# Opening of a two-layer graph attention kernel: four score row buffers, conversions placed behind the ids, first adjacency loads of the second phase in row buffers, and later loads in the first phase's loop

## The chip, the cores and the metric

The kernel runs on one core of a Trainium2 chip. The metric is the device time of one execution in microseconds, as the median of several runs. The engines are TensorE (PE in the profile, its weight loads PEld), VectorE (DVE), ScalarE (ACT), GpSimd (POOL) and SyncE (SP, which here only issues DMAs).

## The reference

Two graph attention layers over 4096 nodes share one adjacency matrix. Its entries are drawn with probability 1/256, made symmetric, and every node is its own neighbour. Cut to what matters:

```python
def reference(x, adj, W_heads, a1, a2, W_out, b_out, W, a):
    # layer 0: 8 heads of 128
    Wh = einsum('nf,hfd->hnd', x, W_heads)
    e = leaky_relu(s1[:, :, None] + s2[:, None, :], 0.2)   # s1 = Wh.a1, s2 = Wh.a2
    att = softmax(where(adj > 0, e, NEG))
    feat = elu(einsum('hnm,hmd->hnd', att, Wh))            # heads side by side
    x = layernorm(x + feat @ W_out + b_out)
    # layer 1: 4 heads of 64, the same form, no output matrix
    ...
    return layernorm(x + h_prime)
```

x is 4096 x 256 in float32, adj is 4096 x 4096 in int32 (64 MB).

## The kernel before, in words

Layer 0 uses that the adjacency is sparse. The 256 groups of 16 target nodes are taken in 8 phases of 32 groups (GP); a phase is 512 rows of adj. For each phase the kernel finds which nodes are neighbours of any target of a group, as lists of ids, and then gathers only those nodes' rows from a table in memory.

The table has one row per node: the 256 numbers of x, a one, two factors per head that come from the node's score (16 numbers), and 32 words. A word says, as a bit mask, which of the 16 targets of one group have this node as a neighbour. There are two tables, and phase s uses table s % 2. The numbers of x are copied into a table by `inputs` (L546, four DMAs of 1 MB, L549). The other 49 words of each row are written by `publish` (L701, DMA L703) from the tile `tail`.

Making a phase's ids has two parts:

- `words_of(s)` (L554) loads the phase's 512 rows of adj in 16 pieces of 512 KB (`load`, DMA L572), converts each to signs in bf16 (`convert`; on DVE for phase 0, L582, on ACT for the others, L584), and sums them with bit weights on PE (`count`, L596), which gives the words. Two buffers hold converted pieces. Phase 0's pieces are loaded into the gather's row buffers (tag "G", 6 buffers), later phases' into three buffers of their own (`aq`). `words_of` returns a list of 19 steps for the later phases; a step loads piece m, converts piece m - 2 and counts piece m - 3.
- `lists_of(s)` (L626) turns the words and picks out the largest candidate numbers, eight at a time (`take`, L673 and L674), merges the four quarters (`merge`, `more`), fills the lists (`fill`, whose copy on ACT is L733), transposes them (`turn`, L738) and writes the tile `ids` (`number`, L751). It returns a list of pieces with a cost each.

The score factors come from class `Scores`. `chunk(k)` makes six steps for each quarter of the nodes: scores on PE (L378), `factors` on DVE and ACT into the tile `row` (L418, L422, L425), transposes of it (`turn`, L433), and `store`. `store` (L439) writes two halves of `row` to the tensor r_d with DMAs issued on ACT (L443), copies the transposed scores (L448, L453), and makes the table's factors on ACT (L454, L457). The publication (L703, on ACT for phase 0) follows. There is one `row` buffer.

Everything up to the end of layer 0 is issued in the order in which the code is written, engine by engine (`manual_schedule`). `opening` (L791) builds phase 0's words and runs phase 0's pieces of `lists_of`; from piece 16 on it takes one score step behind each piece, and behind pieces 24, 26, 31, 33, 35 and 37 one step of the second phase's words (the queue `firsts`). So these loads and conversions stand between the pieces that lead to the ids. Then the first gathers are issued and the loop over groups starts at L1209.

In the loop, group n gathers the rows of group n + 5 (`gather`, L882 on POOL, four DMAs of 128 rows), weighs its own rows on DVE (`weigh`: L987 to L1002, into four buffers with tag "e"), and multiplies on PE (`gathered`, L1010). One more gather per four groups fetches rows shared by them (class `Shared`, L897), and every eight groups the tile of their own rows and score rows is loaded on SP (class `Near`, L940 and L944). Between these the loop takes

- two steps of `firsts` a group; when they are out, `turn_phase(1)` puts the second phase's pieces on the queue `picks`;
- from group 10 (FIRST_COUNT) of phase 0 one step a group of the third phase's words (the queue `counts`); from group 4 (COUNT) in later phases;
- pieces from `picks` as far as a budget per group allows (FIRST 3.0, later EXTRA 2.5, less what the group itself is reckoned at); what is left in group 24 of a phase is run at once;
- in group 27 of each phase `turn_phase` for the phase after next;
- in groups 5, 9, 13 and 17 the copies of x into the second table.

Layer 1 then runs densely over all pairs, bounded by PE. It is not touched by the change.

Of the kernel before, what the change touches and what calls it, by code (L numbers as in the profile page):

```python
# [9 lines left out]
F32 = mybir.dt.float32  # L10
# [8 lines left out]
P = 128  # L19
# [243 lines left out]
def fast_path(  # L263
# [34 lines left out]
    NB = NQ0  # L298
# [37 lines left out]
    class Scores:  # L336
# [29 lines left out]
        def chunk(self, k, src):  # L366
# [41 lines left out]
            def factors():  # L408
                if k == 0:
                    nc.vector.tensor_copy(self.mx[:, 0:1], held["pm"])  # L410
                    nc.vector.tensor_scalar(
                        self.mx[:, 1:2], self.mx[:, 0:1], -1.0, None, ALU.mult
                    )
                ps = held["ps"]
                row = held["row"] = small.tile(
                    [P, HC], F32, tag="row", name=f"row_{n}_{k}", bufs=1
                )
                nc.vector.tensor_scalar(  # L418
                    row[0 : 2 * DQ], ps[0 : 2 * DQ], self.mx[0 : 2 * DQ, 0:1], SPREAD,
                    ALU.add, ALU.min,  # L420
                )
                nc.scalar.activation(  # L422
                    row[2 * DQ :], ps[2 * DQ :], AF.Identity, bias=self.mx[2 * DQ :, 1:2]
                )
                nc.scalar.activation(  # L425
                    row[0 : 2 * DQ], row[0 : 2 * DQ], AF.Exp, scale=1.0 - SLOPE
                )
# [118 lines left out]
    def inputs(i, k):  # L546
        if k == 0:
            nc.sync.dma_start(table[i][N : N + 1, :], zero)
        nc.sync.dma_start(table[i][ts(k, CH), 0:F], x[ts(k, CH), :])  # L549

    lists = [None] * NPH
    words = {}

    def words_of(s):  # L554

        pw = []
        raw, bins = {}, {}
        HN = QN // 2
        NW = PT * NQ0
        PQ = NQ0 // 2  # L560

        def load(m):

            k, t, q = m // (PT * PQ), m // PQ % PT, m % PQ
            if s == 0:
                G = gpool.tile([P, NB, RW], F32, tag="G", name=f"Ga_{m}")
                v = G.rearrange("p b w -> p (b w)")[:, 0 : 2 * HN].bitcast(I32)
                raw[m] = v.rearrange("p (a n) -> p a n", a=2)
            else:
                raw[m] = apool.tile([P, 2, HN], I32, tag="aq", name=f"aq_{s}_{m}")  # L570
            queue = nc.scalar if s == 0 and m % 2 else nc.sync
            queue.dma_start(  # L572
                raw[m],
                adj[ts(s * PT + t, P), ts(k * PQ + q, 2 * HN)].rearrange(
                    "p (a n) -> p a n", a=2
                ),
            )

        def convert(m):
            mb = two.tile([P, 2, HN], BF16, tag="mb", name=f"mb_{s}_{m}", bufs=2)  # L580
            if s == 0:
                nc.vector.tensor_scalar(mb, raw.pop(m), 0.0, 0.5, ALU.is_gt, ALU.subtract)  # L582
            else:
                nc.scalar.activation(mb, raw.pop(m), AF.Sign, bias=half[:, 0:1])  # L584
            bins[m] = mb

        def count(m):


            k, t, q = m // (PT * PQ), m // PQ % PT, m % PQ  # L590
            if t + q == 0:
                pw.append(ps_0.tile([P, HN], F32, tag="o2", name=f"pw_{s}_{k}", bufs=1))
            mb = bins.pop(m)
            for a in range(2):
                r = ts(2 * q + a, GP)
                nc.tensor.matmul(  # L596
                    pw[k][r, :],
                    word[:, t, :],
                    mb[:, a],
                    start=(t == 0),  # L600
                    stop=(t == PT - 1),
                    tile_position=(0, (2 * q + a) * GP),
                    skip_group_check=True,
                )
            if t == PT - 1 and q == PQ - 1:
                if k == 0:
                    words[s] = two.tile([P, QN], F32, tag="ws", name=f"ws_{s}", bufs=2)

                nc.scalar.activation(
                    words[s][:, ts(k, HN)],  # L610
                    pw[k],
                    AF.Identity,
                    bias=half[:, 1:2],
                    scale=1.0 if s == 0 else 0.5,
                )

        lag = 5 if s == 0 else 2

        def piece(m):
            for f, mm in ((load, m), (convert, m - lag), (count, m - lag - 1)):  # L620
                if 0 <= mm < NW:
                    f(mm)

        return [lambda m=m: piece(m) for m in range(NW + lag + 1)]
# [166 lines left out]
    def opening():  # L791
# [19 lines left out]
        for k, (scores, pull, top, factors, turn, store) in enumerate(chunks):  # L811
# [3 lines left out]
            scored.add(turn, lambda k=k, store=store: (store(), publish(k, NCH)))  # L815
            if k == 0:
                scored.add(lambda: near.update({0: Near(0)}))
        firsts.add(*words_of(1))
        for m, (cost, piece) in enumerate(pieces[:-2]):
            piece()  # L820
            if m == 2:
                sc0.weights(a0_sb, w0T_sb)
                chunks[0][0]()
            elif m > 15:
                scored.some()

            if m in (24, 26, 31, 33, 35, 37):
                firsts.some()
        picks.add(*pieces[-2:])
        return firsts  # L830

# [337 lines left out]
    EXTRA = 2.5  # L1169
    FIRST = 3.0  # L1170
    COUNT = 4
    FIRST_COUNT = 10
    rows, shared, near, sums, means = ({} for _ in range(5))
    counts, picks = Late(), Late()

# [19 lines left out]
    with tc.manual_schedule():  # L1195
# [10 lines left out]
        shared[0].copy(near[0].rb)  # L1206
        shared[0].split()
        shared[0].weigh()
        for n in range(NG + SOON + 1):  # L1209
            i, o, s = n // GT, n % GP, n // GP  # L1210
            busy = 0.0
            if n < NG:
                if n == 2:
                    nc.sync.dma_start(w_sb, w0f.rearrange("(c p) d -> p c d", p=P))
                elif n == 4:
                    nc.sync.dma_start(wo_sb, w_out.rearrange("(h d) f -> d h f", d=D0))
                    nc.sync.dma_start(b_sb, b_out)
                if o == (COUNT if s else FIRST_COUNT) and s + 2 < NPH:
                    counts.add(*words_of(s + 2))
                if o == GP - AHEAD - 3:  # L1220
                    while picks.items:
                        picks.items.pop(0)[1]()
                if o == GP - AHEAD and s + 2 < NPH:
                    counts.all()
                    turn_phase(s + 2)
                if n % SL == 0 and n + 2 * SL < NG:
                    shared[n // SL + 2] = Shared(n // SL + 2)
                if n + AHEAD < NG:
                    rows[n + AHEAD] = gather(n + AHEAD)
                if n % GT == 0:  # L1230
                    if i + 1 < NT:
                        near[i + 1] = Near(i + 1)
                    aT = two.tile([P, KC, H0, P], F32, tag="aT", name=f"aT_{i}")
                if n % 4 == 1 and 0 < n // 4 <= NCH:
                    inputs(1, n // 4 - 1)
            if SOON <= n < NG + SOON:
                po, to = sums.pop(n - SOON)
                invert(n - SOON, po)
# [345 lines left out]
```

## Time and profile before

| | us |
|---|---|
| median of 3 runs | 2545.72 (2536.66 to 2552.91) |
| the profiled execution | 2237.41 |
| its span | 2235.6 |
| first gather (L897) starts | 85.67 |
| last gather (L882) starts | 1476.9 |

In the span PE is busy for 89%, DVE for 87%, ACT for 39% and POOL for 48%; the mean granted TensorE clock is 0.957. The profiled execution is shorter than the runs that are timed.

How to read the lines. In a timeline a line gives the start and the time in us, the engine, the source line, the operation, what it writes and reads with the shape, and how many were merged; in square brackets stands how long the engine had been idle before it and what ended that. A group line gives count, busy time, mean ns of one, and the idle time before. An engine's name with a q (ACTq, SPq) is its queue issuing a DMA. POOL's gathers are issued by the engine itself.

### The profile page before, as it was taken

What the parts mean: (1) busy time and instruction counts of PE and PEld (TensorE: products, weight loads), DVE (VectorE), ACT (ScalarE), POOL (GpSimd) and SP (SyncE); (2) the same over time, 40 slices, a digit from 0 to 9 for tenths busy, and PEclk for the clock granted to TensorE, in tenths of its full rate; (3) what the DMA queues carried; (4) which work ended last, traced back from release to release, by engine and by line L of the source; (5) the groups of instructions that cost most, each with busy time, mean ns of one, the idle gap of its engine ahead of it and who ended that gap; (6) DMA issues with size and microseconds to landing.
All of it is one profiled execution on the core that took longest, in us unless ns stands there. A gap on an engine that the chain in (4) does not pass through costs nothing.

```text
span 2235.6 us, 35623 instructions
## 1 busy us (share of the span) xinstructions
PE 1996.7 (89%) x12481; PEld 1142.5 (51%) x12481; DVE 1955.2 (87%) x4117; ACT 882.9 (39%) x1826; POOL 1077.9 (48%) x1154
## 2 busy tenths in 40 slices
PE   5487888989989999989888899888999999999996
PEld 2255566666666666666665667664424333333332
DVE  6579899999989999988999988747998899999996
ACT  1333424424334334334432233234445444465563
POOL 1377777777777777777777777730000000000000
PEclk9589999989999999999999999999999999999998
DMA  9799677578567677667665555538665566676762
GB/s 323 192 297 258 180 206 245 152 198 249 158 178 239 180 182 231 192 178 216 205 143 150 150 153 139 147 114 298 218 196 191 168 216 217 204 229 223 224 211 87
DMA packets 184149, 443.55 MB, mean 198 GB/s; under 512 B 60788, under 2 KB 92535, under 8 KB 183959
## 3 DMA queue, kind: packets, MB, share of 16 engines
q1 hardware_dynamic: 125814, 265.99, 37.9%
q0 software_dynamic: 52224, 169.97, 27.8%
q10 hardware_dynamic: 5920, 5.21, 0.8%
q8 instruction: 101, 1.65, 0.3%
q14 instruction: 90, 0.73, 0.1%
HBM read 426.04 MB, written 23.40 MB: 201 GB/s over the span
## 4 chain that ended last, share of the span: by engine, by line
PE 44%; DVE 33%; DMA 11%; issue 4%; POOL 4%; ACT 2%; SPq 1%; DVEq 0%; ACTq 0%; POOLq 0%
PE po L1327 20%; PE po L1339 10%; PE po L1010 9%; DMA G<-table,ids 7%; DVE e L988 5%; DVE e L994 5%; DVE e L1002 5%; POOL G L882 4%; DVE side L987 2%; DVE side L996 2%; PE py L1093 1%; DVE lst L673 1%; PE pw L858 1%; DVE hT L1084 1%; DVE side L916 1%
## 5 line engine op out<-in xcount | busy, mean ns | idle before, releaser
L882 POOL DMA_INDIRECT G<-table,ids x1024 | 977.9, 955 | 319.0 <-issue 234.1
L1496 DVE SCALAR_TENSOR_TENSOR e<-rb,pj,mb 128x1024 f32<-128x1024 f32 x512 | 635.5, 1282 | 58.9 <-PE po L1339 27.8
L1010 PE MATMUL po<-G,e 128*128 128x257 f32 x2048 | 553.5, 416 | 75.9 <-DVE e L1002 75.6
L1327 PE MATMUL po<-e,wh 128*32 128x512 f32 x4096 | 531.3, 595 | 7.1 <-DVE e L1496 7.1
L1010 PEld LDWEIGHTS po<-G,e 128*128 128x128 f32 x2048 | 392.1, 201 | 222.2 <-DVE e L1002 119.8
L1309 ACT ACTIVATE mb<-aq 128x1024 bf16<-128x1024 int32 x256 | 271.1, 1061 | 321.5 <-DVE e L1496 264.4
L1339 PE MATMUL po<-e,cj 128*32 128x512 f32 x2048 | 315.2, 594 | 0.0
L1411 POOL TENSOR_SCALAR nm<-nm 128x4 f32<-128x4 f32 x6 | 5.5, 911 | 640.6 <-ACT ju L1410 640.6
L1327 PEld LDWEIGHTS po<-e,wh 128*32 128x32 f32 x4096 | 149.7, 110 | 290.9 <-issue 252.6
L1034 ACT ACTIVATE ag<-po,rd_all 128x256 f32<-128x256 f32 x256 | 121.5, 475 | 321.0 <-DVE rd_all L1030 317.0
L1044 ACT COPY aT<-pa 128x256 f32<-128x256 f32 x256 | 94.8, 370 | 377.9 <-PE pa L1041 371.1
L1010 PE MATMUL po<-own,eo 128*128 128x257 f32 x512 | 166.3, 407 | 62.5 <-ACT ag L1034 57.8
L988 DVE TENSOR_TENSOR e<-rb,side 128x512 f32<-128x512 f32 x256 | 175.8, 687 | 9.1 <-DVE side L987 0.3
L994 DVE TENSOR_TENSOR e<-e,side 128x512 f32<-128x512 f32 x256 | 175.7, 686 | 8.9
L1002 DVE TENSOR_TENSOR e<-e,side 128x512 f32<-128x512 f32 x256 | 175.7, 686 | 8.8
L1010 PE MATMUL po<-Gs,e_s 32*128 32x257 f32 x512 | 182.0, 435 | 1.5 <-DVE e_s L931 1.5
L1070 PE MATMUL ph<-aT,w_sb 128*128 128x128 f32 x1024 | 145.6, 287 | 11.8 <-DVE hT L1084 11.6
L1339 PEld LDWEIGHTS po<-e,cj 128*32 128x32 f32 x2048 | 80.3, 110 | 147.3 <-issue 135.2
L1070 PEld LDWEIGHTS ph<-aT,w_sb 128*128 128x128 f32 x1024 | 135.1, 199 | 26.4 <-DVE hT L1084 12.4
L584 ACT ACTIVATE mb<-aq,half 128x1024 bf16<-128x1024 int32 x112 | 128.6, 1151 | 36.4 <-issue 18.6
L1093 PE MATMUL py<-wo_sb,hT 128*128 128x256 f32 x512 | 125.4, 388 | 0.0
L1010 PEld LDWEIGHTS po<-Gs,e_s 32*128 32x128 f32 x512 | 76.0, 185 | 89.3 <-issue 87.1
(171 smaller groups left out, 1907.3 us busy)
## 6 DMA issues: line engine op xcount, KB each, us to landing
aq<-in_adjT SPq DMA_DIRECT2D x256, 512.0 KB
aq<-in_adj SPq DMA_DIRECT2D x112, 512.0 KB
rb<-r_d SPq DMA_DIRECT2D x48, 512.0 KB
G<-table,ids POOLq DMA_INDIRECT x1024, 3.4
table<-in_x SPq DMA_DIRECT2D x8, 1024.0 KB
table<-tail SPq DMA_DIRECT2D x56, 98.0 KB
own<-table SPq DMA_DIRECT2D x32, 152.5 KB
Ga<-in_adj SPq DMA_DIRECT2D x8, 512.0 KB
```

What stands on the lines that cost most here:

```text
L584: nc.scalar.activation(mb, raw.pop(m), AF.Sign, bias=half[:, 0:1])
L882: nc.gpsimd.indirect_dma_start(out=G[:, b, :], out_offset=None, in_=table[s % 2][:, :], in_offset=bass.IndirectOffsetOnAxis(ap=lists[s][:, ...
L988: nc.vector.tensor_tensor(e, rb[:, :, ts(n % GT, T)].unsqueeze(1).to_broadcast(sh), f_p[:, :, 0:H0].unsqueeze(3).to_broadcast(sh), ALU.mult,)
L994: nc.vector.tensor_tensor(e, e, f_p[:, :, H0:].unsqueeze(3).to_broadcast(sh), ALU.max)
L1002: nc.vector.tensor_tensor(e, e, nb_p.unsqueeze(2).to_broadcast(sh), ALU.mult)
L1010: nc.tensor.matmul(po, w.rearrange("p h t -> p (h t)"), v[:, 0 : F + 1], start=first, **kw)
L1070: nc.tensor.matmul(phs[k][:, hh, :], w_sb[:, c, ts(h, D0)], aT[:, c, h, :], start=(c == 0), stop=(c == KC - 1),)
L1093: nc.tensor.matmul(pys[0], hT[:, h, :], wo_sb[:, h, :], start=False, stop=(h == H0 - 1))
L1309: nc.scalar.activation(mb, aq, AF.Relu, scale=OPEN)
L1327: nc.tensor.matmul(po[q][ts(b, DQ), :], wh[:, j, k, d : d + DQ], es[k][:, ts(q, HB)], start=(j == 0), stop=(j == NT - 1), tile_position=(0 ...
L1339: nc.tensor.matmul(po[NQ][r0 : r0 + DQ, :], sc1.cj[:, j, 2 * g + k : 2 * g + k + 1].to_broadcast([P, DQ]), es[k][:, ts(q, HB)], start=(j = ...
L1496: nc.vector.scalar_tensor_tensor(e, rb[k], sc1.pj[:, j, h : h + 1], mb, ALU.max, ALU.min)
```

## The change

- The `row` tile of layer 0's scores comes from the pool tag "e" with four buffers, which the loop uses for its weights later. Layer 1's scores keep their single buffer.
- For the second phase `words_of` takes another form. Seven pieces (EARLY) are loaded at once, pieces 0 to 2 into the three `aq` buffers and pieces 3 to 6 into gather row buffers. The other nine are loaded as `aq` buffers come free: piece m + 7 behind the conversion of piece m for m below 3, piece m + 3 behind it for m from 7 on. It returns 16 steps, each a conversion, a count and such a load.
- In `opening` the steps are made when the score steps are all taken, which is behind piece 30. None of them runs there. Seven run behind the first gathers and the first weights of the shared and own rows, ahead of the loop; the other nine run two a group in the loop.
- FIRST_COUNT is 13 instead of 10, the copies of x into the second table stand in groups 10, 14, 18 and 22, and `turn_phase(2)` stands in group 31 of phase 0 instead of 27.

```diff
@@ factors
-                row = held["row"] = small.tile(
-                    [P, HC], F32, tag="row", name=f"row_{n}_{k}", bufs=1
-                )
+                if n == 0:
+                    row = two.tile([P, HC], F32, tag="e", name=f"row_{n}_{k}", bufs=4)
+                else:
+                    row = small.tile([P, HC], F32, tag="row", name=f"row_{n}_{k}", bufs=1)
+                held["row"] = row
@@ words_of
+    EARLY = 7
...
-            if s == 0:
-                G = gpool.tile([P, NB, RW], F32, tag="G", name=f"Ga_{m}")
+            if s == 0 or (s == 1 and 3 <= m < EARLY):
+                G = gpool.tile([P, NB, RW], F32, tag="G", name=f"Ga_{s}_{m}")
...
+        if s == 1:
+            def then(m):
+                convert(m)
+                count(m)
+                k = m + EARLY if m < 3 else m + 3 if m >= EARLY else NW
+                if k < NW:
+                    load(k)
+
+            for m in range(EARLY):
+                load(m)
+            return [lambda m=m: then(m) for m in range(NW)]
@@ opening
-        firsts.add(*words_of(1))
         for m, (cost, piece) in enumerate(pieces[:-2]):
             piece()
...
-            if m in (24, 26, 31, 33, 35, 37):
-                firsts.some()
+            if not scored.items and not firsts.items:
+                firsts.add(*words_of(1))
@@ the loop over groups
-    FIRST_COUNT = 10
+    FIRST_COUNT = 13
...
         shared[0].weigh()
+        firsts.some(EARLY)
         for n in range(NG + SOON + 1):
...
-                if o == GP - AHEAD and s + 2 < NPH:
+                if o == (GP - AHEAD if s else GP - 1) and s + 2 < NPH:
                     counts.all()
                     turn_phase(s + 2)
...
-                if n % 4 == 1 and 0 < n // 4 <= NCH:
-                    inputs(1, n // 4 - 1)
+                if n % 4 == 2 and 2 <= n // 4 < 2 + NCH:
+                    inputs(1, n // 4 - 2)
```

## The prediction

> **What bounds the kernel now.** I read the page first (its slices, then its groups), then POOL's timeline with its waits, then the timeline of the opening on all engines, and last the chain of waits through the opening, with the landing times of its DMAs.
>
> From the page: the span, the busy line, and the group that gathers rows.
>
> ```profile
> span 2235.6 us, 35623 instructions
> PE 1996.7 (89%) x12481; PEld 1142.5 (51%) x12481; DVE 1955.2 (87%) x4117; ACT 882.9 (39%) x1826; POOL 1077.9 (48%) x1154
> ...
> POOL 1377777777777777777777777730000000000000
> ...
> L882 POOL DMA_INDIRECT G<-table,ids x1024 | 977.9, 955 | 319.0 <-issue 234.1
> ```
>
> Row POOL: its sevens begin in slice 2 and stop in slice 28, which is layer 0. A gather takes 0.95 us and is followed by 0.30 us of issue, so 1.25 us is its period and seven tenths is a full POOL. 1024 gathers of L882 and 64 of L897 need 1088 x 1.25 = 1360 us; in POOL's timeline the first starts at 85.67 and the last ends at 1478, 1392 us. Only 32 us are lost over eight phases of 32 groups. DVE is nearly as full (about 46.8 us of each 50 us from 185 on, by windows), PE too. So layer 0 is a chain of gathers: when it starts and what POOL loses on the way set its end. Layer 1 (1485 to 2235) runs behind it on PE and is not touched.
>
> When it starts is set by the opening. From its timeline:
>
> ```profile
> 55.09 0.74 DVE L418 TENSOR_SCALAR row<-ps,mx 64x512 f32<-64x512 f32 x1 [4.32 <-DMA r_d<-row]
> 59.77 0.26 ACT L454 ACTIVATE tail<-dc 128x64 f32<-128x64 f32 x1 [2.51 <-DMA table<-in_x]
> 61.33 0.74 DVE L418 TENSOR_SCALAR row<-ps,mx 64x512 f32<-64x512 f32 x1 [2.37 <-DMA r_d<-row]
> 70.59 0.74 DVE L418 TENSOR_SCALAR row<-ps,mx 64x512 f32<-64x512 f32 x1 [5.40 <-DMA r_d<-row]
> 75.04 0.39 ACTq L703 DMA_DIRECT2D table<-tail  x1
> 83.06 1.15 ACT L584 ACTIVATE mb<-aq,half 128x1024 bf16<-128x1024 int32 x1 [4.35 <-DMA aq<-in_adj]
> 84.11 0.15 ACT L733 COPY lst<-pf 128x8 f32<-128x8 f32 x1
> 85.07 0.30 DVE L751 TENSOR_SCALAR ids<-pl 128x136 int32<-128x136 f32 x1 [4.58 <-PE pl L740]
> 85.67 1.21 POOL L897 DMA_INDIRECT Gs<-table,ids  x1 [77.48 <-DMA aq<-in_adj]
> ```
>
> Two stalls stand before the ids. One row buffer makes L418 wait three times for the store of the chunk before: 4.32 + 2.37 + 5.40 = 12.1 us. And a conversion (L584) that waits for its adjacency load stands on ACT ahead of the small copy L733, which the ids need.
>
> The chain shows what those DMAs stand behind:
>
> ```profile
> 39.01 20.42 DMA table<-in_x
> 59.45 1.75 DMA r_d<-row
> 63.83 6.64 DMA r_d<-row
> ```
>
> The last of four 1 MB copies of x into the table lands at 59.43. The same 8 KB store takes 1.75 us on quiet queues and 6.64 us beside three adjacency loads.
>
> **What the Trainium skill says.** "DMA: Bandwidth & Descriptors", Anatomy of one DMA: a DMA engine waits for no semaphore; the issuing sequencer does, before it dispatches. The trace agrees, and it matters here: L454 waited 2.51 us for a copy into the table, with which it shares no data. The program gives the DMAs of SP and ACT eight completion semaphores in turn, and an issue waits for the last DMA on its semaphore; the second store of chunk 1 waited for the fourth table copy, and all of ACT with it. Same page, Queues, rings and completion order: each engine goes round between the queues it has work for, so ACT's stores share with SP's loads; 1.75 against 6.64 us agrees. Same page, Specifications: under 512 B a transfer is below line rate. A publication of the table's tail (L703) has rows of 49 words, 196 B, and landed 4.5 us after its issue with little beside it (the fourth, at 79.55) and 7.4 to 10.3 us in traffic. "TensorE: Matmul & The Clock Gate", Part 1: an idle PE falls to half rate; the 16 matmuls of L378 take 3.64 us at 57 and 1.92 at 48.
>
> **The change part by part.** Sums are against the profiled execution, 2237.4 us, span 2235.6. The median of the runs shown, 2545.7, is 308 us longer, and no view shows where; I carry the same microseconds over to it.
>
> *Four row buffers.* No instruction is added. The direct gain is the 12.1 us. But the work on ACT behind those rows keeps its own waits. L418 of chunk 1 moves from 55.09 to 50.77, and its first store (2.19 us later, as now) to 53.0. The second store still shares a semaphore with the table copy of 59.43 if the program hands them out in the present order, so ACT continues at 59.45 as now. Chunk 2's L422 then runs at 60.6 instead of 62.15, and its transposed scores reach DVE (L448) at about 62, not 57: 4.8 of the 12.1 us are a wait for ACT.
>
> *Seven loads at once instead of three.* They are issued when the scores are done in program order, but SP has nothing else to do after 60.1, so they go out there, 3.67 MB. The first three landed at 65.91, 68.75 and 70.44 before, 2.27 us apart; at that pace the fourth lands at 72.7, the fifth at 75, the seventh at 79.5. They take semaphores between those of chunks 1 to 3. With eight in turn, chunk 2's publication comes round to that of chunk 1 (landed 69.93 before), and chunk 3's to the fifth load. So ACT publishes chunk 2 at 70, runs L422 of chunk 3 at 70.4 (71.74 before), and publishes chunk 3 at about 75.1, as now (75.04). DVE takes chunk 3's scores at 71.7 instead of 73.21, a gain of 1.5.
>
> *Conversions behind the ids.* L733 follows L725 at once. From chunk 3's scores to the end of the last L674 of the merge is 7.3 us now (73.21 to 80.49); then some 0.7 us for L733, the transposes and L751: the ids at 71.7 + 7.3 + 0.7 = 79.7. The first gather could go 0.6 us later, as now, at 80.3. It also needs the publication of 75.1 in the table: landing after 4.5 to 9.7 us, 79.6 to 84.8. I take 82, a gain of 3.7. The seven conversions (1.15 us, 8.1 us together) now follow four copies on ACT; the gathers of groups 2 to 4 must wait for three of the borrowed row buffers. Group 2's gathers come 10 periods, 12.5 us, after the first; the fourth conversion is done some 5 us after it. Hidden; were a load 8 us late, POOL would stand for the excess. On PE 14 matmuls of 0.3 us come before the first group, in time in which PE waits for its first rows.
>
> *The rest of the second phase's words.* Nine items at two a group instead of thirteen: its lists start in group 4, not 6, and by the code's own costs only 2.0 us, not 4.1, are left to be flushed in group 24.
>
> *Table copies of x in groups 10 to 22 instead of 5 to 17; third phase's loads from group 13 instead of 10.* Now SP issues both at 128 to 191 beside the second phase's publications, and POOL waits for gathers that land late:
>
> ```profile
> 158.08 0.94 POOL L897 DMA_INDIRECT Gs<-table,ids  x1 [2.04 <-DMA G<-table,ids]
> 174.41 0.94 POOL L882 DMA_INDIRECT G<-table,ids  x1 [2.12 <-DMA G<-table,ids]
> 254.29 0.94 POOL L882 DMA_INDIRECT G<-table,ids  x1 [2.06 <-DVE side L916]
> ```
>
> Phase 0 takes POOL 264.3 - 87.2 = 177.1 us, the next six 173.8 on average. Spread out, I bring it to the others: 3.3 us, 4 with part of the last wait. Bounds: 0 (the copies only collide later) to 7 (the minimum of 170). On SP each moved copy stands in order before own rows and score rows; group 22's copy, issued at about 215, lands within 18 us (the slowest of now), by 233, and is needed at about 258.
>
> *Third phase's lists from group 31 instead of 27.* No work goes; four groups of it move from phase 0, where DVE is up to 24 us behind POOL, into phase 1. By the code's costs 4.8 us remain to be flushed at group 56, where now nothing does. POOL asks for these ids at about 422, DVE reaches the flush 4.8 us earlier than now (415) and needs some 6. Taken at nothing; at most 5 us.
>
> **Sum.** Opening 3.7, phase 0 about 4: 8 us, 2229 in the profile, 2538 in the timed runs.
>
> **The rivals.**
> *The whole opening is won.* If the semaphores fall otherwise (the seven loads after the last store), ids come at 85.07 - 12.1 - 3.9 = 69.1 and POOL starts at 70: 16 us, with phase 0 20 to 25, 2523. For it: nothing but that order makes ACT wait. Against: in the program of before, SP's loads were already placed ahead of ACT's stores that stand before them in the code.
> *Nothing is left.* DVE trails POOL by 20 to 24 us from group 24 on (L987 against the gather of its rows), as far as six buffers allow; a POOL that starts earlier then waits for buffers. Time 2546. Against: DVE starts earlier too, and the trail is 3 us at the end.
> *Slower.* The table's last publication is queued behind the seven loads. If it shares the semaphore of the last load (79.5) and lands 9.7 us later, POOL starts at 89.8, 4 us later than now, with nothing won in phase 0: 2550. It decides from a landing after 85.1 on. For it: publications of 9.7 us in traffic; against: traffic ends with the loads.
>
> **How the numbers follow.** Forecast 0.42, whole opening 0.28, nothing 0.19, slower 0.11. One per cent is 25 us, about what a measurement of this kernel can tell from no change. The first rival reaches it only with phase 0's full 7 us and some of the loop's start (DVE waits 5.9 us for rows at 114.9): 0.15. Slower by that much needs a stall on POOL that recurs: 0.05. The range runs from 2516 (opening and loop won, and the runs' own spread of 8 us) to 2556 (slower, with the same spread).
>
> **What would show it.** L418's waits on r_d gone, in their place a wait on L448; ACT held before L454 until 59.4; first gather between 79 and 85; POOL from there to group 32 in about 174; no wait of POOL over 1 us in groups 2 to 4 or near group 56. A first gather near 70, or after 86, shows the forecast wrong.

## The result, and the profile after

The changed kernel took 2536.94 us (median of 22 runs, 2525.96 to 2543.41), the kernel before 2544.72 us beside it (22 runs): a ratio of 0.9969, 95% interval 0.9955 to 0.9984. That is 7.8 us less; 8 were forecast. It is a third of the 1% that the prediction reckoned can be told from no change, but the interval leaves out 1.

The profile of before that the prediction used (2237.41 us) came from a chip on which layer 0 runs about 300 us faster than on the chip of the timed runs, whatever the kernel, as the experiments show. So each comparison below stays with one kind of chip, called a 2237 us chip and a 2544 us chip after the median of the kernel before; where two chips of one kind are compared, the text says so.

The profile after came from a 2544 us chip. Its page, in the lines that answer to those of before (lines of code have moved: L882 is L897 now, L897 is L912, L418 is L420, L422 is L424, L443 is L445, L448 is L450, L454 is L456, L703 is L720, L584 is L587, L751 is L768):

```profile
span 2535.0 us, 35632 instructions
PE 2132.3 (84%) x12481; PEld 1218.0 (48%) x12481; DVE 1964.2 (77%) x4117; ACT 872.5 (34%) x1826; POOL 1079.5 (43%) x1154
...
POOL 1566666566555666565656666665000000000000
...
L897 POOL DMA_INDIRECT G<-table,ids x1024 | 981.0, 958 | 608.3 <-issue 258.7
```

The gathers take what they took (958 ns), but POOL has fives and sixes where it had sevens, and 608.3 us of idle time before them instead of 319.0. The same kernel, run later on a 2237 us chip (e9_after_again), gives the page that can be laid against the one of before:

```profile
span 2227.6 us, 35632 instructions
PE 1992.7 (89%) x12481; PEld 1141.2 (51%) x12481; DVE 1953.9 (88%) x4117; ACT 883.2 (40%) x1826; POOL 1075.8 (48%) x1154
...
POOL 1377777777777777777777777730000000000000
...
L897 POOL DMA_INDIRECT G<-table,ids x1024 | 977.2, 954 | 316.9 <-issue 234.8
```

Here POOL is full from slice 2 to slice 28, as before, and the span is 8.0 us shorter. By POOL's timeline the first gather starts at 83.46 (85.67 before, 2.2 us earlier) and the last at 1469.5 (1476.9 before, 7.4 us earlier). In this pair 2.2 us were won up to the first gather and 5.2 us on the way through layer 0; 0.6 us comes behind the last gather. But e9_after_again is late before it reaches any line that the change touches: its first row tile is made at 47.29 us, at 45.09 in the profile of before. Four more kernels below have the same opening on 2237 us chips (e5, e6, e7 and e11), and their first gathers start at 80.64 to 81.35, 4.3 to 5.0 us earlier than before. Counted from the first row tile, e9_after_again also wins 4.4 us. So the opening is worth 4 to 5 us there, and of the 7.4 us some 3 are left for the loop.

The opening itself, from the timeline of all engines of e9_after_again:

```profile
53.40 0.73 DVE L420 TENSOR_SCALAR row<-ps,mx 64x512 f32<-64x512 f32 x1
55.59 4.52 ACTq L445 DMA_DIRECT2D r_d<-row  x2
57.18 0.73 DVE L420 TENSOR_SCALAR row<-ps,mx 64x512 f32<-64x512 f32 x1
60.16 0.26 ACT L456 ACTIVATE tail<-dc 128x64 f32<-128x64 f32 x1 [4.60 <-DMA table<-in_x]
62.37 0.23 DVE L450 COPY d<-pr 128x64 f32<-128x64 f32 x1 [2.62 <-PE pr L435]
63.67 0.73 DVE L420 TENSOR_SCALAR row<-ps,mx 64x512 f32<-64x512 f32 x1
68.07 0.68 ACT L424 ACTIVATE row<-ps,mx 64x512 f32<-64x512 f32 x1 [4.49 <-DMA aq<-in_adj]
69.53 0.23 DVE L450 COPY d<-pr 128x64 f32<-128x64 f32 x1 [3.20 <-PE pr L435]
72.43 0.39 ACTq L720 DMA_DIRECT2D table<-tail  x1
76.66 0.30 DVE L768 TENSOR_SCALAR ids<-pl 128x136 int32<-128x136 f32 x1
83.46 1.21 POOL L912 DMA_INDIRECT Gs<-table,ids  x1 [75.17 <-DMA aq<-in_adj]
```

L420 waits for nothing any more. But ACT needs 4.52 us to issue the two stores of chunk 1, since the second stands behind the fourth table copy, and then L456 and, a chunk later, L424 wait 4.60 and 4.49 us for DMAs with which they share no data. DVE meets those waits at L450. The ids are done at 76.96, and yet the first gather starts 6.5 us later: the last publication (L720, issued at 72.43) lands at 82.49 by the semaphore updates in the trace. The line names a load instead, which landed at 83.33 and was issued behind the gather in the code. That the publication is what POOL waits for shows over the runs: in all ten profiles in which it lands after the ids are done, the first gather starts 0.92 to 0.97 us after its landing; in the other four it starts 0.30 us after the ids. In the profile after, from the other kind of chip, the line says so itself:

```profile
78.79 1.21 POOL L912 DMA_INDIRECT Gs<-table,ids  x1 [70.58 <-DMA table<-tail]
...
480.57 0.95 POOL L912 DMA_INDIRECT Gs<-table,ids  x1 [8.43 <-DVE ids L768]
```

There the publication took 4.76 us instead of 10.06; the seven profiles of kernels with this opening lie between these two. The second line is a stall that the change brought: the gather of the third phase's first shared rows, which is issued in group 56, waits 8.43 us for that phase's ids (3.66 us in e3_one_row below, and not at all in the kernels with the lists from group 27).

### The profile page after: what moved, and what is told of

Its sections match the earlier page's. It is cut to its first block, busy times and chain, and to the rows that moved or that the text cites. A ratio compares the mean times of both kernels' runs of the same rounds, so it can differ in the third digit from the quotient of the medians.

```text
span 2535.0 us, 35632 instructions
## 1 busy us (share of the span) xinstructions
PE 2132.3 (84%) x12481; PEld 1218.0 (48%) x12481; DVE 1964.2 (77%) x4117; ACT 872.5 (34%) x1826; POOL 1079.5 (43%) x1154
## 4 chain that ended last, share of the span: by engine, by line
PE 65%; another core or an unknown queue 13%; ACT 8%; DVE 6%; issue 5%; DMA 2%; POOL 1%; SPq 0%; ACTq 0%; DVEq 0%; POOLq 0%
PE po L1025 27%; PE po L1343 17%; PE po L1355 9%; PE py L1108 3%; PE ph L1085 3%; ACT mb L587 2%; PE pa L1056 2%; ACT ag L1049 1%; ACT rb_s L924 1%; PE pw L873 1%; PE pw L599 1%; ACT aT L1059 1%; DMA Ga<-in_adj 1%; ACT el L1096 1%
## 5 line engine op out<-in xcount | busy, mean ns | idle before, releaser
L897 POOL DMA_INDIRECT G<-table,ids x1024 | 981.0, 958 | 608.3 <-issue 258.7
L1025 PE MATMUL po<-G,e 128*128 128x257 f32 x2048 | 621.3, 455 | 16.9 <-issue 11.5
L1025 PEld LDWEIGHTS po<-G,e 128*128 128x128 f32 x2048 | 433.0, 222 | 185.0 <-issue 67.6
L1025 PE MATMUL po<-own,eo 128*128 128x257 f32 x512 | 186.6, 449 | 224.1 <-ACT ag L1049 173.2
L1044 DVE TENSOR_SCALAR rd_all<-po 128x1 f32<-128x1 f32 x256 | 38.7, 151 | 238.6 <-PE po L1025 139.2
L1025 PEld LDWEIGHTS po<-own,eo 128*128 128x128 f32 x512 | 85.7, 210 | 252.4 <-ACT ag L1049 190.6
L1025 PE MATMUL po<-Gs,e_s 32*128 32x257 f32 x512 | 202.2, 478 | 3.8 <-DVE e_s L943 3.8
L1085 PE MATMUL ph<-aT,w_sb 128*128 128x128 f32 x1024 | 153.8, 292 | 26.4 <-issue 15.3
L1085 PEld LDWEIGHTS ph<-aT,w_sb 128*128 128x128 f32 x1024 | 140.6, 204 | 43.1 <-issue 25.7
L1025 PEld LDWEIGHTS po<-Gs,e_s 32*128 32x128 f32 x512 | 84.1, 204 | 102.9 <-issue 98.4
```

Of the source, the lines that this page charges most:

```text
L897: nc.gpsimd.indirect_dma_start(out=G[:, b, :], out_offset=None, in_=table[s % 2][:, :], in_offset=bass.IndirectOffsetOnAxis(ap=lists[s][:, ...
L1025: nc.tensor.matmul(po, w.rearrange("p h t -> p (h t)"), v[:, 0 : F + 1], start=first, **kw)
L1085: nc.tensor.matmul(phs[k][:, hh, :], w_sb[:, c, ts(h, D0)], aT[:, c, h, :], start=(c == 0), stop=(c == KC - 1),)
```

## The experiments

Kernels e1 to e4 ran on a 2544 us chip (before: 2543.55 us), e5 to e8 on a 2237 us chip (before: 2237.24), e9 to e12 on another of these (before: 2236.87). In the diffs, - is the changed kernel.

### The kernel before, once more (e1_before_again)

No edit.

> The kernel before, unchanged, for a second profile. The changed kernel's profile shows 105 us for 16 groups of gathers in layer 0 and a span of 2535 us, the first profile of before 87 us and 2236 us, at a granted TensorE clock of 0.895 and 0.957. If that is a state of the chip and no effect of the change, this run shows a clock near 0.895, a span near 2540 us and 104 to 108 us for 16 groups, with the first gather at 85.7 as in the first profile. If it is the change, this run is at 2236 us again.

2534.0 us, span 2532.2 at a granted clock of 0.899, against 2535.0 and 0.895 of the profile after. So the 300 us belong to the chip and not to the change. Its first gather starts at 83.61, 4.8 us later than in the changed kernel there. That its single run is 2.8 us shorter than the changed kernel's, while the medians differ by 7.8 us the other way, shows that single spans settle nothing on this chip (its runs spread over 17 us for the changed kernel and 40 us for the one before).

### The four row buffers alone (e2_rows_alone)

```diff
-        if s == 1:
...
-        firsts.some(EARLY)
+        firsts.add(*words_of(1))
...
+            if m in (24, 26, 31, 33, 35, 37):
+                firsts.some()
```

with the three later placements undone, so that the second phase's words have their old form.

> Only the four row buffers, all else as before. Theory A (the time follows the first gather, and ACT's own waits eat part of what the row buffers free): L418's 12.1 us of waits go, chunk 2's scores come at about 62 and chunk 3's at about 67 since ACT is held before L454, the conversion in front of L733 still waits for its load, first gather at 78 to 81; 5 to 7 us faster than before. Theory B (the gain of the change is in the loop, the opening is absorbed by DVE or PE later): the first gather comes earlier, but the time is within 2 us of before. Theory C (the row buffers take all 12.1 us): first gather at 73.5, 12 us faster.

2539.26 us, ratio 0.9991 (0.9969 to 1.0013): no difference that can be told from zero. The first gather is at 79.72, 3.9 us earlier than in e1_before_again; whether that arrives at the end these runs do not show.

### All but the four row buffers (e3_one_row)

```diff
-                if n == 0:
-                    row = two.tile([P, HC], F32, tag="e", name=f"row_{n}_{k}", bufs=4)
...
+                row = held["row"] = small.tile(
+                    [P, HC], F32, tag="row", name=f"row_{n}_{k}", bufs=1
+                )
```

> The changed kernel with the single row buffer of before. Theory A: the waits of L418 are back, and longer, since seven loads are in flight instead of three (7 to 12 us for a store instead of 6.6): 4 + 3 + 9 = 16 us of waits; the conversions are out of L733's way (3.9 us won); first gather at 83 to 88, time between 1 us faster and 4 us slower than before. Theory B: the gain of the loop stays, 6 to 8 us faster than before. Theory C: 3.9 us faster.

2537.83 us, ratio 0.9975 (0.9955 to 0.9995). The first gather is back at 84.11, and still 5.7 us are won. The rows make the opening's gain, and on this chip most of the total, by the medians, comes from elsewhere.

### The later placements undone (e4_early_again, e11_early_again2)

```diff
-    FIRST_COUNT = 13
+    FIRST_COUNT = 10
...
-                if o == (GP - AHEAD if s else GP - 1) and s + 2 < NPH:
+                if o == GP - AHEAD and s + 2 < NPH:
...
-                if n % 4 == 2 and 2 <= n // 4 < 2 + NCH:
-                    inputs(1, n // 4 - 2)
+                if n % 4 == 1 and 0 < n // 4 <= NCH:
+                    inputs(1, n // 4 - 1)
```

> The changed kernel with the third phase's loads, the table copies and the third phase's lists where they were before (from group 10; in groups 5, 9, 13, 17; in group 27). Theory A: first gather at 78 to 80 as in the changed kernel, and nearly the whole gain stays: 5 to 8 us faster than before. Theory B: the gain goes, within 2 us of before. My prediction's sum: 4 us of the 8 go.

> The changed kernel with the three later placements undone (third phase's loads from group 10, its lists from group 27, copies of x in groups 5 to 17). Theory: 3 to 5 us faster than the changed kernel on the same chip, 11 to 13 us below before, all of it in groups 32 to 64. Rival (the later placements help phase 0 by as much as they cost in phase 1): equal within 1 us.

On the 2544 us chip 2531.78 us, ratio 0.9954 (0.9933 to 0.9976); against the rows alone (0.9991) this puts the new form of the second phase's words at about 9 us (the runs of the two kernels differ by 9.0 us in the mean, 95% interval 3 to 15 us), and DVE's first phase (first weights of group 0 to those of group 32) shrinks by as much, from 233.8 to 224.7 us. POOL's does too. Its first gathers for groups 0 and 32, in e2_rows_alone (where the line is L884) and then in e4_early_again:

```profile
81.24 0.95 POOL L884 DMA_INDIRECT G<-table,ids  x1 [0.30 <-issue]
296.24 0.94 POOL L884 DMA_INDIRECT G<-table,ids  x1 [2.13 <-DVE rd_all L1031]
```

```profile
80.69 0.95 POOL L897 DMA_INDIRECT G<-table,ids  x1 [0.30 <-issue]
285.09 0.94 POOL L897 DMA_INDIRECT G<-table,ids  x1 [0.30 <-DVE y L1114]
```

That is 215.0 against 204.4 us. The other profiles from 2544 us chips fall in with these: 216.7 us with the old form (e1_before_again), 202.2 with the new one (the changed kernel and e3_one_row). And from 84 to 300 us ACT stands idle before its conversions for 51 and 55 us in the two kernels with the old form, 22 to 25 in the three with the new one; on the 2237 us chips for 31 us in the kernel before and 9 to 13 in the eight others. That these waits on ACT are what held the loop fits all of this, but no run changes them alone.

On the 2237 us chip 2228.27 us, ratio 0.9957 (0.9945 to 0.9969), beside 2230.07 and 0.9969 (0.9959 to 0.9979) of the changed kernel: 1.8 us apart, less than the 3 to 5 expected and less than the intervals resolve. No help from the three later placements together shows on either chip. A cost is seen as a wait only at group 56 of the 2544 us chip; that two of them cost time on the 2237 us chips too comes out with e12_lists27_pool below.

### The changed kernel on the other chip (e9_after_again)

> The changed kernel as it is, taken together with three variants against one run of the kernel before. Theory (most of the gain is in the first phase of the loop, and the second phase gives part of it back at the flush in group 56): 6 to 9 us below before, the stretch from group 32 to 64 (DVE) 7 to 11 us longer than in the other lists-27 variants. If the give-back had been only a matter of the other chip, this one is within 2 us of the variants without it, that is 11 to 13 us below before.

2230.07 us, ratio 0.9969 (0.9959 to 0.9979), 6.8 us less: the same ratio as on the 2544 us chip. The level is the theory's, and so is the second phase by DVE, 179.0 us against 169.1 in e11_early_again2, though at the end only 1.8 us lie between these two kernels. The lists from group 31 move work from the first phase into the second, as the windows of the two show (length, then busy time and instructions of PE, PE's loads, DVE, ACT, POOL, then clock, DMA share, GB/s). Before:

```profile
96.60:290.30 193.70, 159.66 (x687) 105.35 (x687) 161.77 (x430) 72.18 (x150) 141.83 (x150) 0.90 0.80 236
290.30:459.20 168.90, 151.66 (x718) 106.59 (x718) 158.35 (x432) 64.60 (x145) 128.26 (x135) 0.97 0.70 200
```

e9_after_again:

```profile
93.10:276.00 182.90, 153.42 (x658) 101.74 (x657) 156.11 (x421) 66.05 (x135) 133.81 (x143) 0.90 0.83 238
276.00:455.10 179.10, 159.54 (x742) 110.95 (x743) 164.08 (x440) 67.94 (x157) 136.63 (x143) 0.96 0.69 195
```

DVE's busy time goes from 161.77 to 156.11 us in the first phase and from 158.35 to 164.08 in the second; both together are 362.6 us long before and 362.0 now. As the rest of the change lies between these two kernels as well, that does not show that the move is free. And here the stall at the second phase's end does not come: the ids are done at 414.4, the gather that needs them goes out at 417.77 behind the usual 0.30 us. The margin has shrunk from 12.0 us (410.1 against 422.1 before) to 3.4.

### The lists at 27, the copies late (e5_lists27)

```diff
-    FIRST_COUNT = 13
+    FIRST_COUNT = 10
...
-                if o == (GP - AHEAD if s else GP - 1) and s + 2 < NPH:
+                if o == GP - AHEAD and s + 2 < NPH:
```

> The changed kernel with the third phase's words from group 10 and its lists from group 27 again; the copies of x stay in groups 10 to 22. Theory D (the changed kernel loses some 9 us in phase 1, because the lists moved to group 31 are not done by group 56 and are flushed there, so that the gathers wait for the ids): the wait of the shared gather in group 56 (8.4 us in the changed kernel) is gone, phase 1 takes 207 to 211 us in DVE's starts instead of 218; 3 to 6 us faster than the changed kernel, 11 to 14 us faster than before. Theory E (the moved copies of x are what costs): phase 1 stays at 216 or more, time as the changed kernel.

2225.44 us, ratio 0.9947 (0.9934 to 0.9960), and the second phase is back at 169.0 us (DVE). The ids of the third phase are at 397.3, 16 us ahead of their gather. Its interval only touches that of e9_after_again, which ran on another 2237 us chip. The same edit is the only difference between e10_after_pool and e12_lists27_pool, which ran on one chip; these show below that it is worth about 4 us.

### A larger budget in the second phase (e6_budget)

```diff
-                spare = pick(spare + (EXTRA if s else FIRST) - busy)
+                spare = pick(spare + (EXTRA if s > 1 else FIRST) - busy)
```

> The changed kernel with the budget of phase 0 (3.0) for the queue of lists in phase 1 too, so that the third phase's lists, begun in group 31, are through before group 56 by the code's costs (nothing left to flush, instead of 4.8 us). Theory D: no wait of the shared gather in group 56 over 2 us, phase 1 at 207 to 212 us, 3 to 6 us faster than the changed kernel. Theory F (it is the work itself, 7 us of DVE, that was moved into phase 1, not the flush): phase 1 stays at 216 to 218 and the time as the changed kernel.

2231.11 us, ratio 0.9967 (0.9952 to 0.9981), 5.7 us more than e5_lists27 on the same chip. The third phase's ids come at 397.1 instead of 414.4, so the budget does free them early, but the second phase stays 178.2 us long. Its length is the moved work and not the flush, and earlier ids bring no gain that shows.

### The second phase's lists held to group 6 (e7_held_to_6)

The edit of e4_early_again, and

```diff
-                    if not firsts.items:
-                        turn_phase(1)
+                if n == 6:
+                    turn_phase(1)
```

> The changed kernel with the third phase's loads, lists and the table copies where they were before, and with the second phase's lists begun in group 6 as before, not in group 4. Theory G (the gain in phase 0 comes half from the lists being through by group 24, so that the flush there and its way through PE and ACT go): groups 22 to 24 take 6 us longer than in the same kernel with lists from group 4, phase 0 at 229 to 232 us instead of 225, time 4 to 7 us slower than that kernel, 5 to 8 us faster than before. Theory H (the gain comes from the conversions being out of the loop's way on ACT): phase 0 stays at 223 to 226.

2229.59 us, ratio 0.9964 (0.9951 to 0.9977), against 2228.27 and 0.9957 without the hold (e11_early_again2, on another 2237 us chip). One microsecond, with DVE's first phase 192.1 against 191.0 us, although the flush is back: from group 23's first weights to group 24's DVE takes 10.9 us, 7.8 without the hold. The two groups by which the lists begin earlier are not the source of the gain. What this profile does show is how large a single late gather can be in the first phase:

```profile
164.66 0.94 POOL L897 DMA_INDIRECT G<-table,ids  x1 [6.24 <-DMA G<-table,ids]
```

### The opening's stores on POOL's queue (e8_early_pool, e10_after_pool, e12_lists27_pool)

The direct test of the prediction's main reason, that ACT is held by issues that wait for other DMAs. The stores and the first phase's publications leave ACT:

```diff
-                    nc.scalar.dma_start(
+                    (nc.scalar if n else nc.gpsimd).dma_start(
...
-            (nc.sync if s else nc.scalar).dma_start(
+            (nc.sync if s else nc.gpsimd).dma_start(
```

in e10_after_pool with nothing else, in e8_early_pool with the edit of e4_early_again, in e12_lists27_pool with that of e5_lists27.

> The kernel with the loads, copies and lists where they were before, and in which the opening's stores and publications are issued on POOL's queue instead of ACT's, so that ACT waits for no DMA's semaphore there. Theory A (ACT's waits for semaphores of other DMAs hold the scores, and the late publication the first gather): L418's and L448's waits both go, ids at 68 to 71 instead of 74.8, first gather at 71 to 75 instead of 78.8, 4 to 7 us faster than with ACT's queue, 16 to 19 us faster than before. Rival (the publications land no sooner for an earlier issue, because the DMA engines are full until 77): ids at 68 to 71, but first gather at 77 to 79 and no change of time.

> The changed kernel with layer 0's score stores and the first phase's publications issued on the queue of POOL instead of ACT's. Theory (ACT's issues stood behind unrelated DMAs): ids about 5 us earlier, first gather 3 to 5 us earlier than in the changed kernel, and about as much at the end: ratio to before 1.5 to 2 thousandths lower, 10 to 14 us below before. Rival (an earlier gather is lost again at the first adjacency-bound stretch): first gather earlier, end within 1 us of the changed kernel's.

> The changed kernel with the third phase's loads from group 10 and its lists from group 27, the copies of x left in groups 10 to 22, and the opening's stores and publications on POOL's queue. If the two gains add, 15 to 17 us below before, the fastest of the four. If they do not add (an earlier start is given back in phase 0), it equals the kernel with the early lists alone, 11 to 13 us below before.

| | us | ratio to before | ids | first gather |
|---|---|---|---|---|
| e9_after_again | 2230.07 | 0.9969 (0.9959 to 0.9979) | 77.0 | 83.46 |
| e10_after_pool | 2226.07 | 0.9948 (0.9934 to 0.9961) | 69.0 | 75.97 |
| e12_lists27_pool | 2221.80 | 0.9929 (0.9915 to 0.9942) | 68.5 | 74.93 |
| e8_early_pool (other chip) | 2221.24 | 0.9933 (0.9914 to 0.9952) | 69.5 | 75.45 |

The ids come 8 us earlier than in e9_after_again (6 to 7.5 earlier than in the four other kernels with its opening), and with that as early as the first rival put them (69.1 by its working). From the timeline of e12_lists27_pool:

```profile
53.88 0.26 ACT L456 ACTIVATE tail<-dc 128x64 f32<-128x64 f32 x1 [0.90 <-DVE dc L455]
60.96 0.22 DVE L450 COPY d<-pr 128x64 f32<-128x64 f32 x1
62.22 0.93 POOL L720 DMA_DIRECT2D table<-tail  x1 [0.26 <-ACT tail L459]
68.17 0.30 DVE L768 TENSOR_SCALAR ids<-pl 128x136 int32<-128x136 f32 x1
74.93 1.08 POOL L912 DMA_INDIRECT Gs<-table,ids  x1 [11.77 <-DMA Ga<-in_adj]
```

ACT's waits for DMAs ahead of the ids are gone, and so is DVE's at L450. The last publication is issued 10 us earlier, at 62.22 instead of 72.43. But it now goes out in the middle of the seven loads, and the first gather starts 12.7 us after its issue, 6.5 us after the ids, the same distance as in e9_after_again. Of 7.5 us by which e10_after_pool gathers earlier (1.9 of them the late start of e9_after_again), 4.0 us arrive at the end (medians; 4.5 in the mean, 95% interval 2 to 7 us); its gathers lose 3.5 us more on the way than those of e9_after_again, by POOL's timelines. With the loads from group 10 and the lists at 27 in addition, e12_lists27_pool is the fastest kernel on its chip, 15.1 us below before and 8.3 us below the changed kernel, with intervals that do not overlap. Loads that wait for the last publication were not tried.

The step from e10_after_pool to e12_lists27_pool is 4.3 us (4.2 in the mean, 95% interval 1 to 7 us). So the later loads and lists together cost about 4 us on this chip, although no gather waits for the third phase's ids in e10_after_pool (done at 408.2, gathered with at 409.39). DVE takes 361.3 us for the first two phases there and 357.3 in e12_lists27_pool; POOL's first two phases are not longer for it (349.8 and 351.1 us), so on which wait the 4 us are lost is open. The copies of x alone make no difference that can be told from zero: kernels that differ only in their place, on two 2237 us chips, are at 0.9957 (early, e11) and 0.9947 (late, e5), and with POOL's queue at 0.9933 (early, e8) and 0.9929 (late, e12).

## Why the prediction was right, and where it was not

**The premise.** That layer 0 is a chain of gathers holds on the chip of the profile: POOL's period is 0.954 + 0.30 us in e9_after_again, and from the second phase on it waits for little else. On the chip of the timed runs it does not hold: POOL there is idle 291 us more before its gathers than in e9_after_again, and TensorE stands for 65% of the chain of work that ended last instead of 45%, by the pages (see the last section). That the same ratio, 0.9969, came out on both chips is luck: the working carried the microseconds over without a reason.

**Four row buffers.** As worked out: the waits of 12.1 us at L418 gone, ACT held before L456 (forecast to 59.4, measured 60.16), chunk 2's scores at DVE at 62.37 (forecast 62), a wait at L450 in their place. (A store is 16 KB by the trace's list of DMA issues, not 8 as the working has it; nothing was computed from that.)

**The seven loads.** The last landed at 80.09 (forecast 79.5), though they did not go out at once: SP issued three by 61.74 and the others at 66.35 to 70.55, three of these 0.06 to 0.07 us after the landing of an earlier DMA on the same semaphore. The order of the semaphores was one off: chunk 2's publication came round to the first load's (landed 67.50) and not to that of chunk 1's publication (71.25), so it left at 67.58, not 70. Hence chunk 3's scores at 69.53 instead of 71.7, and the ids at 76.96 instead of 79.7; the 8.0 us from those scores to the ids were 7.4.

**The publication behind the loads.** Taken as 4.5 to 9.7 us with a landing that lets the gather go at 82. In e9_after_again it left 2.7 us earlier than forecast and took 10.06 us, and the gather went at 83.46: a gain of 2.2 instead of 3.7 us, or 4.4 without the late start of that profile. In the four other kernels with this opening on 2237 us chips it took 5.9 to 9.5 us, and the gather went at 80.64 to 81.35 (taken as 82). On the other chip it took 4.76 us, and the gain is 4.8 us (83.61 to 78.79). So the term was about right, a little small, with two errors that offset each other: an earlier issue, and a landing near or beyond the end of the range. The slower rival's place was the right one to watch: with 0.97 us from landing to gather, the landing at 82.49 is 2.2 us from the one that would have won nothing.

**Phase 0.** Here a step failed. The moved copies of x and the later loads were to take away the late gathers at 158 and 174 and bring POOL's first phase from 177.1 to about 174. It took 176.5 us, and the waits are still there:

```profile
155.54 0.94 POOL L912 DMA_INDIRECT Gs<-table,ids  x1 [1.07 <-DMA G<-table,ids]
175.93 0.95 POOL L897 DMA_INDIRECT G<-table,ids  x1 [2.60 <-DMA G<-table,ids]
178.29 0.94 POOL L897 DMA_INDIRECT G<-table,ids  x1 [1.41 <-DMA G<-table,ids]
```

5.1 us of waits, against 4.2 us in the two lines of before. Nor is it this one profile: between the nine profiles from 2237 us chips, what POOL's pauses over 0.5 us in the first phase exceed the usual 0.30 us by sums to 2.2 to 6.5 us with the copies at 5 to 17 (four kernels) and to 3.6 to 7.0 us with the copies at 10 to 22 (five). The place of the copies is not what makes gathers late; what does is open. What did go is the wait for DVE at 254.29 (2.06 us), and group 24 with its flush takes DVE 7.9 us instead of 10.9: the earlier second phase's lists, which the prediction noted (2.0 instead of 4.1 us to flush) and priced at nothing. By e7_held_to_6 that price was about right.

**What came in its place.** In the pair of profiles from 2237 us chips, the 5.2 us between first and last gather lie in POOL's pauses and periods of several phases: 0.6 us in the first, 1.5 in the second, 2.7 in the fourth, 1.1 in the sixth, the others within 0.5. That is one profile against one, and two kernels with the same loop differ by 3.3 us in the first phase (174.3 in e5_lists27, 177.6 in e12_lists27_pool), so what won time in the loop on these chips is open. On the 2544 us chip the experiments split it more clearly: rows about 2 us, the new form of the words about 9 (0.9991 to 0.9954), the later placements about 4 against it (0.9954 to 0.9969, the latter beside other runs of before); each of these is uncertain by several us. The first phase there, 215 to 217 us with the old form and 202 to 204 with the new one, shows it without such doubt. So the forecast's 4 us of phase 0 had about the right size for the net and the wrong part of the change for its cause: the evidence puts it with the words, whose new form the prediction priced at nothing in the loop, and no run shows a gain from the later placements.

**Lists from group 31.** Taken at nothing, at most 5 us, as a wait for the ids. On the 2237 us chips there was no such wait (margin 3.4 us in e9_after_again), but with the later loads the move costs about 4 us all the same (e10_after_pool against e12_lists27_pool): that it is free was the second step that failed. On the timed chip the wait was 8.43 us, over the bound: the margin was reckoned with the pace of the 2237 us profile.

**Hidden parts.** No gather waited over 1 us in groups 2 to 4, as forecast.

**The sum.** 8 us forecast; 7.8 and 6.8 us measured. Of the three terms the first was 3.7 against 4 to 5. The second was 4 from the later copies and loads, which no run shows to help; what won time in its place, on the 2544 us chip, was the new form of the words, about 9 us. The third was 0 against a cost of about 4 us on the 2237 us chips and a wait of 8.43 us in the profile after. That these came to 8 is luck in good part.

## What to carry to other kernels

Where DMAs are issued by an engine that also computes, read the waits of that engine for releasers with which it shares no data; here moving eight stores and four publications to an idle engine's queue brought the ids 8 us forward and the end 4. Follow the data to its landing and not to its issue: an earlier publication amid bulk loads arrived late all the same. Do not take moved work as free because no wait appears where it goes: here it cost about 4 us. And a gain that is worked out from one profile should be tried against a chip in another condition before a margin is called slack: 12 us of slack became an 8.43 us stall.

## What the runs showed of the hardware

Nearly all of the 300 us between the chips lie in layer 0: the last gather starts at 1767.4 us in the profile after and at 1469.5 in e9_after_again, and what follows takes 767.6 and 758.1 us. There the granted clock of TensorE is lower. Windows of the profile after, then of e9_after_again, the same columns as above:

```profile
690.00:860.00 170.00, 142.62 (x616) 98.71 (x615) 127.40 (x341) 53.10 (x133) 104.69 (x110) 0.88 0.56 162
1900.00:2100.00 200.00, 200.00 (x1812) 72.26 (x1803) 173.48 (x148) 96.59 (x174) 0.00 (x0) 1.00 0.60 197
```

```profile
690.00:860.00 170.00, 153.20 (x722) 107.37 (x721) 159.04 (x434) 64.71 (x145) 129.35 (x137) 0.97 0.71 200
1900.00:2100.00 200.00, 200.00 (x1854) 61.15 (x1850) 191.53 (x161) 110.98 (x195) 10.08 (x16) 1.00 0.69 222
```

In layer 0 TensorE was granted 0.88 against 0.97 and got through 616 matmuls instead of 722 in 170 us; in layer 1, where it never rests, both have 1.00. The clock is granted in stretches at full or at half rate: in the 170 us the profile after has seven at half rate, 41 us in all, and e9_after_again three, 10 us. Such a stretch and the one behind it in the profile after, and pairs of matmuls in them:

```profile
700.80:707.50 6.70, 5.06 (x11) 3.20 (x12) 3.45 (x9) 2.16 (x7) 3.78 (x4) 0.50 0.33 93
707.70:731.40 23.70, 18.73 (x100) 12.68 (x100) 18.23 (x47) 5.46 (x20) 16.45 (x17) 1.00 0.37 98
```

```profile
702.44 1.22 PE L1025 MATMUL po<-own,eo 128*128 128x257 f32 x2 [4.48 <-ACT ag L1049]
703.59 1.22 PE L1025 MATMUL po<-Gs,e_s 32*128 32x257 f32 x2
...
710.44 0.69 PE L1025 MATMUL po<-Gs,e_s 32*128 32x257 f32 x2
```

The Trainium skill, "TensorE: Matmul & The Clock Gate", Part 1, says that an idle TensorE falls to half rate, and this agrees: TensorE had rested 4.48 us up to 702.44, and the same pair takes 1.22 us in the stretch at 0.50 and 0.69 us in the one at 1.00. It suggests a loop that feeds itself: a late matmul makes the next engines late, TensorE rests longer, and is slow again. No run tests that, and why one chip stays in it and another does not was not settled here.
